# 480 columns instead of 512 for the lower half of the ninth tap, in a float32r convolution layer split over two row tiles

## The chip, the cores and the metric

The kernel runs on one core of a Trainium2 chip. The metric is the device time of one execution in microseconds. Three runs of the kernel before gave 2569.12, 2569.26 and 2569.37 us (median 2569.26). Beside them there is a profile of one execution. The mean granted clock of TensorE in it is 1.000 of full speed.

## What is computed

The input x is 4 images of 32 x 32 pixels with 16 channels. Four residual layers follow each other, each on a group-normalized x. Three of them (0, 1 and 3) are the same kind of position-dependent convolution; cut down:

```python
first   = einsum('ijyx,byxc->bijc', M, x)
kern    = G as (h*w*f, c, 3, 3)              # one 3x3 kernel for every output pixel (i,j) and f
shifted = conv(x, kern, padding='SAME')      # 1024*16 output channels over 32x32 pixels
diff    = relu(x - shifted)                  # for every (i,j): an image of 32x32
second  = einsum('ijyx,bijyxc->bijc', W, diff)
x       = x + first - second
```

Layer 3 names pixels and sums the other way round, and comes to the same work. Layer 2 is an interval network (running maxima and minima over rows and columns, two dynamic-programming steps with sigmoids, and a linear map), small beside the others.

## The kernel before

**Phases, chunks, steps.** The batch is cut into two groups of two images (g = 0, 1). A phase is one convolution layer for one group: six phases. A phase has 8 chunks of 128 output pixels (t), and a chunk has 32 steps, one for each output channel f and image b. In the very first chunk the steps are sorted by groups of four f and then by b (four steps of b = 0, then four of b = 1); in all others b changes with every step. There are 6 x 8 x 32 = 1536 steps.

**A step.** It computes, for 128 output pixels, the image x - shifted of 32 x 32 = 1024 pixels with the sign turned, in two PSUM banks of 512 columns: bank h of the pair `ps[:, h, :]` is half h of the image, 16 rows of 32 pixels. The contraction runs over 9 taps x 16 channels = 144 rows. Eight taps are spread over two slots of four taps (64 partitions each), and the ninth tap has a slot of its own. The partitions 0 to 63 and 64 to 127 hold the two halves of the image, so that each matmul has 64 rows and the two halves run on two row tiles of the systolic array. `products` (L582) issues for every weight and image operand two matmuls, h = 0 on partitions 0 to 63 and h = 1 on partitions 64 to 127; such a pair is called a pass here.

**Precision.** Weights and images are split into an upper and a lower part so that float32r products give enough of float32. In all but the first 16 steps `first_part` (L597) issues four passes (`iy` for two slots, `iz` for two slots), then ScalarE scales the two banks in place (L618). `second_part` (L621) issues two passes of `iyz` and one of the ninth tap, `im9` with `W9`. So a step has seven passes. The first 16 steps (`u < PLAIN`) use plain float32 products of `raw` for the eight taps, and float32r for the ninth.

**Order.** It is written out by hand. `conv_layer` issues the first part of step n+1, then the second part of step n. VectorE then takes min(ps, 0) times the layer's W over the 1024 columns and sums along them (L634), which gives one output column. There are four pairs of banks. In the gaps between steps, generators are advanced: `prep_parts` makes the next weights on ScalarE, VectorE and POOL and sends the halves that have to change partitions through SP's queue; `behind` does the normalization, the interval network and the image operands of the next phase.

**Image operands.** `before_conv` (L338) writes the normalized image, padded to 34 x 34, to DRAM (`xs`), and reads it back as shifted windows into `raw`, one DMA for each tap and half, both images of the group in one (L359). `RUN` is the length of such a window: 15 rows of 34 and one of 32. The ninth tap is stored four times (four rows of 16 channels) because its operand is split in precision over them. `split`, `difference`, `halve` and `halve_rest` make `iy`, `iz`, `iyz` and `im9` from it.

**The ninth tap.** It is the one at the lower right of the 3 x 3 window. For the image's last row of pixels (row 15 of half 1) it reads only the zero padding below the image.

**The start.** For phase 0 the host has laid the windows out (`xi`), not normalized. The kernel normalizes them in place (`normal`, L807) and then has to set the padding to zero again: `sides` (L794) multiplies a window's left and right column and top and bottom row by masks of 0 and 1 per partition (`kept`, made at L739 to L750 from the table `outside`), and clears the ninth tap's right column and, for half 1, its last row with memsets (L798, L799).

Of the kernel before, what the change touches and what calls it, by code (L numbers as in the profile page):

```python
# [16 lines left out]
B, H, C = 4, 32, 16  # L17
NG = 2
GB = B // NG
# [4 lines left out]
HP = H + 2  # L24
NPP = HP * HP
HI = H // 2
PITCH = HI * HP
NH = HI * H
RUN = (HI - 1) * HP + H
ROWS = P // H  # L30
FU = 4
NU = C // FU
# [9 lines left out]
def net_kernel(ctx: ExitStack, tc: tile.TileContext, x, xq, xi, convs, iv_w, iv_b, out):  # L42
# [58 lines left out]
    raws, units, chunks = {}, {}, {}  # L101
# [7 lines left out]
    def load_chunk(n):  # L109
        if n < n_chunks:  # L110
            t = n % NT
            chunks[n] = wpool.tile([P, NP], F32, tag="WT", name=f"WT_{n}")
            nc.sync.dma_start(chunks[n], convs[phases[n // NT][1]][1][t * P : (t + 1) * P, :])
# [5 lines left out]
    raw = const.tile([P, 3, GB, PITCH], F32, name="raw")  # L119
    iy = [const.tile([P, 2, GB, NH], F32R, name=f"iy{g}") for g in range(NG)]  # L120
    iz = [const.tile([P, 2, GB, NH], F32R, name=f"iz{g}") for g in range(NG)]
    iyz = [const.tile([P, 2, GB, NH], F32R, name=f"iyz{g}") for g in range(NG)]
    im9 = [const.tile([P, GB, NH], F32R, name=f"im9{g}") for g in range(NG)]
# [3 lines left out]
    first = big.tile([P, 8192], F32, tag="big", name="first")  # L127
# [3 lines left out]
    def load_plain(eng, u, at, to):  # L131
        src = convs[0][2][0, u]
        eng.dma_start(raws[u][:, ::2, at:to], src[:, :2, at:to])
        for h in range(2):
            eng.dma_start(
                raws[u][64 * h : 64 * h + 64, 1, at:to], src[64 - 64 * h : 128 - 64 * h, 0, at:to]
            )

    load_plain(nc.scalar, 0, 0, F0)
    for slot in (0, 2, 1):  # L140
        nc.sync.dma_start(raw[:, slot, 0, :RUN], xi[0][:, slot, :RUN])
    load_chunk(0)
    load_plain(nc.sync, 0, F0, FU)
    nc.sync.dma_start(raw[:, :, 1, :RUN], xi[1][:, :, :RUN])
    load_plain(nc.sync, 1, 0, FU)
# [40 lines left out]
    def image(v, x):  # L186
        return v.rearrange("... (y x) -> ... y x", x=x)[..., :H]
# [68 lines left out]
    def split(eng, g, b, name, pause=IDLE):  # L256

        high = upper(image(raw[:, :2, b], HP), 2, f"x{name}{b}")
        yield 1
        for s in range(2):  # L260
            eng.tensor_tensor(
                image(iz[g][:, s, b], H), image(raw[:, s, b], HP), image(high[:, s], H), ALU.subtract
            )
            yield pause
            nc.scalar.activation(iy[g][:, s, b], high[:, s], AF.Copy, scale=EPS)
# [72 lines left out]
    def before_conv(g, layer):  # L338
        xn = work.tile([P, NT, GC], F32, tag="xn", bufs=2, name=f"xn_{g}_{layer}")
        xns[g] = xn  # L340
        yield from group_norm(g, f"c{g}{layer}", xn, 1 if layer == 2 else 4)

        nc.vector.transpose(
            xt[g][:, :, 1 : 1 + H], xn
        )
        inner = xs[g][:, HP : HP + H * HP].rearrange("p (t r n) -> p r t n", r=ROWS, n=HP)
        for r in range(ROWS):
            nc.sync.dma_start(inner[:, r], xt[g][GC * r : GC * (r + 1)])  # L350
        yield 2
        xsv = xs[g].rearrange("(b c) n -> c b n", b=GB)
        for slot, row, tap in [(tap // 4, tap % 4, tap) for tap in range(8)] + [
            (2, row, 8) for row in range(4)
        ]:
            for h in range(2):
                off = (HI * h + tap // 3) * HP + tap % 3
                r0 = 64 * h + C * row
                nc.sync.dma_start(  # L359
                    raw[r0 : r0 + C, slot ^ h if slot < 2 else 2, :, :RUN], xsv[:, :, off : off + RUN]  # L360
                )
            yield 1
        yield 6 if layer == 2 else 12
        for b in range(GB):
            yield from split(nc.gpsimd, g, b, f"{g}{layer}")
            yield IDLE
            halve(image(im9[g][:, b], H), image(raw[:, 2, b], HP), low_x)
            for s in range(2):
                difference(nc.gpsimd, g, b, s)
            yield 3  # L370
            halve_rest(image(im9[g][:, b], H), image(raw[:, 2, b], HP), low_x)
            yield 1
# [73 lines left out]
    def interval_layer(g):  # L446
# [18 lines left out]

        raw = one[:GC].rearrange("p (j t r) -> p r t j", j=H, r=ROWS)
        for row in range(ROWS):
            if row == 2:
# [110 lines left out]
        yield 1  # L579


    def products(ps, pairs, first):  # L582


        for k, (w, v) in enumerate(pairs):
            for h in range(2):
                r = slice(64 * h, 64 * h + 64)
                nc.tensor.matmul(  # L588
                    ps[:, h, :],
                    lhsT=w[r],  # L590
                    rhs=v[r],
                    start=first and k == 0,
                    stop=k == len(pairs) - 1,
                    skip_group_check=not first,
                )

    def first_part(step):  # L597
        phase, t, f, b = step
        g = phases[phase][0]
        n = phase * NT + t  # L600
        u = n * NU + f // FU
        ps = bank_pair(f"pc_{n}_{f}_{b}")
        if u < PLAIN:
            products(
                ps,
                [(raws[u][:, s, f % FU], image(raw[:, s, b], HP)) for s in range(2)]
                + [(units[u][3][:, f % FU], im9[g][:, b])],
                True,
            )
            return ps  # L610
        WU, WL, WD, W9 = (w[..., f % FU, :] for w in units[u])
        products(
            ps,
            [(WU[:, s], iy[g][:, s, b]) for s in range(2)]
            + [(WL[:, s], iz[g][:, s, b]) for s in range(2)],
            True,
        )
        nc.scalar.activation(ps, ps, AF.Copy, scale=1.0 + EPS)  # L618
        return ps

    def second_part(step, ps):  # L621

        phase, t, f, b = step
        g = phases[phase][0]
        n = phase * NT + t
        u = n * NU + f // FU
        if u >= PLAIN:
            WU, WL, WD, W9 = (w[..., f % FU, :] for w in units[u])
            products(
                ps, [(WD[:, s], iyz[g][:, s, b]) for s in range(2)] + [(W9, im9[g][:, b])], False  # L630
            )
        col = b * C + f
        junk = work.tile([P, NP], F32, tag="junk", name=f"junk_{n}_{col}")
        nc.vector.scalar_tensor_tensor(  # L634
            junk,
            ps.rearrange("p h n -> p (h n)"),
            0.0,
            chunks[n],
            op0=ALU.min,
            op1=ALU.mult,  # L640
            accum_out=accs[phase][:, t, col : col + 1],
        )
        if (f, b) == (C - 1, GB - 1):
            acc = accs[phase][:, t]
            if n == 0:
                plain_acc = acc.rearrange("p (b c) -> p b c", c=C)[:, :, : PLAIN * FU]
                nc.vector.tensor_scalar_mul(plain_acc, plain_acc, EPS)
            if phase < len(phases) - 1:
                nc.gpsimd.tensor_scalar_mul(acc, acc, 1.0 / EPS)  # L649
                nc.gpsimd.tensor_tensor(X[g][:, t], X[g][:, t], acc, ALU.add)  # L650
            else:
                nc.vector.scalar_tensor_tensor(
                    X[g][:, t], acc, 1.0 / EPS, X[g][:, t], op0=ALU.mult, op1=ALU.add
                )
                if t == NT - 2:
                    nc.sync.dma_start(out[g][:, : NT - 1], X[g][:, : NT - 1])
# [55 lines left out]
    pairs = const.tile([P, C // 2], F32, name="pairs")  # L712
# [13 lines left out]
    for b in range(GB):  # L726
# [3 lines left out]
    rows = const.tile([P, 2, 4], F32, name="rows")  # L730
# [3 lines left out]

    outside = {
        "left0": (rows[:, 0, 0::3], rows[:, 1, 2:3]), "right0": (rows[:, 0, 2:3], rows[:, 1, 1:2]),
        "top0": (rows[:, 0, 0:3],), "bottom0": (rows[:, 1, 2:4],),
        "left1": (rows[:, 0, 2:3], rows[:, 1, 0::3]), "right1": (rows[:, 0, 1:2], rows[:, 1, 2:3]),
    }  # L739
    kept = const.tile([P, len(outside) + 4], F32, name="kept")  # L740
    keep = {}
# [23 lines left out]
    ps = bank("ps_own")  # L765
# [28 lines left out]
    def sides(eng, b, slot):  # L794

        v = raw[:, slot, b].rearrange("p (y x) -> p y x", x=HP)
        if slot == 2:
            eng.memset(v[:, :, H - 1 : H], 0.0)  # L798
            eng.memset(v[64:, HI - 1, :H], 0.0)  # L799
        for side, at in (  # L800
            ("left", v[:, :, 0]), ("right", v[:, :, H - 1]),
            ("top", v[:, 0, :H]), ("bottom", v[:, HI - 1, :H]),
        ):
            if f"{side}{slot}" in keep:
                eng.tensor_scalar_mul(at, at, keep[f"{side}{slot}"])  # L805

    def normal(eng, b, slot):  # L807
        v = raw[:, slot, b, :RUN]
        if eng is nc.scalar:
# [127 lines left out]
```

## Time and profile before

| | us |
|---|---|
| median of three runs | 2569.26 (2569.12 to 2569.37) |
| span of the profiled execution, first to last instruction | 2566.6 |
| TensorE matmuls busy (L588 and others) | 2552.4, 99% of the span |
| TensorE weight loads busy | 2064.8 |
| VectorE busy | 2079.7 |
| ScalarE busy | 1894.8 |
| POOL busy | 1102.1 |
| matmuls of the ninth tap (im, W), 3072 of them | 622.6, 396 ns each |
| matmuls of iy, iz, iyz, 6080 of each | 966 to 968 each, 392 to 393 ns each |

The profiled execution is one execution recorded by the hardware; the page gives its span, and no other total for it. What lies before the first and after the last instruction is in the timed runs but not in the span: 2569.26 - 2566.6 = 2.7 us.

How to read it: busy time of matmuls is a sum of intervals whose ends are modelled and which overlap, as two row tiles work at once and a matmul begins before the results of the last have drained. So a share of 99% doesn't say that the array is full. Starts are recorded. The distance between the starts of successive passes is therefore the measure used here. A line of the timeline merges neighbouring instructions of one kind ("x4" are two passes of two halves): its first number is the start of the first, its second the time until the end of the last. PE's weight loads (PEld) are shown apart from its matmuls. A wait is put down to the instruction whose end released it.

### The profile page before, as it was taken

Reading aid. Unit: us, or ns where it says so; the run is one execution under the profiler, and the core shown is the slowest. Engines: PE = TensorE matmul, PEld = TensorE weight load, DVE = VectorE, ACT = ScalarE, POOL = GpSimd, SP = SyncE. Lnnn points to the kernel's source line nnn. Section 1 sums busy time; section 2 is a strip of 40 time slices with the busy share of each in tenths; the row PEclk is TensorE's granted clock in tenths of the full one; section 3 lists DMA queues with packets and bytes.
Section 4 is the critical chain, followed back from the end, with each engine's and each line's share of the span. In section 5 each row is a group of like instructions: output and inputs, shape, how many; then the busy total and the mean of one; then the engine's idle time right before and its main releaser. Section 6 shows DMA issues by size and latency. Waiting matters only on the chain.

```text
span 2566.6 us, 56663 instructions
## 1 busy us (share of the span) xinstructions
PE 2552.4 (99%) x21906; PEld 2064.8 (80%) x21906; DVE 2079.7 (81%) x3620; ACT 1894.8 (74%) x2181; POOL 1102.1 (43%) x991
## 2 busy tenths in 40 slices
PE   8999999999999999999999999999999999999999
PEld 5998888888888887888888877788878887788887
DVE  9887777888777887777788888888888887777777
ACT  4777777777777777777777777777777777777776
POOL 3445333453333434333345554454646344333332
PEclk9999999999999999999999999999999999999999
DMA  5656344464444654444454444554444466344442
GB/s 170 187 144 170 108 132 140 114 167 136 128 136 128 194 159 120 136 129 128 132 140 132 132 116 133 140 156 130 122 132 133 130 161 198 110 141 132 132 132 52
DMA packets 81182, 353.80 MB, mean 138 GB/s; under 512 B 18448, under 2 KB 20368, under 8 KB 80144
## 3 DMA queue, kind: packets, MB, share of 16 engines
q1 hardware_dynamic: 79920, 349.57, 48.7%
q8 instruction: 172, 2.82, 0.4%
q14 instruction: 98, 0.80, 0.1%
q10 hardware_dynamic: 864, 0.58, 0.1%
q0 software_dynamic: 128, 0.02, 0.0%
HBM read 199.19 MB, written 0.98 MB: 78 GB/s over the span
## 4 chain that ended last, share of the span: by engine, by line
PE 99%; ACT 0%; DVE 0%; issue 0%; POOL 0%; DVEq 0%; ACTq 0%; POOLq 0%
PE pc L588 98%; PE pf L387 1%; ACT pc L618 0%; PE ps_l L510 0%; PE ps_r L523 0%; DVE junk L634 0%; ACT L323 0%; DVE raw L805 0%; PE ps_y L574 0%; DVE kept L748 0%; ACT L553 0%; PE ps_v L758 0%; DVE raw L813 0%; DVE kept L744 0%; DVE squares L781 0%
## 5 line engine op out<-in xcount | busy, mean ns | idle before, releaser
L634 DVE SCALAR_TENSOR_TENSOR junk<-pc,WT 128x1024 f32<-128x1024 f32 x1536 | 1879.7, 1224 | 461.7 <-PE pc L588 416.2
L618 ACT ACTIVATE pc<-pc 128x1024 f32<-128x1024 f32 x1520 | 1531.8, 1008 | 637.2 <-PE pc L588 607.4
L588 PE MATMUL pc<-iyz,parts 64*128 64x512 f32 x6080 | 966.5, 393 | 1.7 <-ACT pc L618 1.7
L588 PE MATMUL pc<-iy,parts 64*128 64x512 f32 x6080 | 967.8, 393 | 0.0
L588 PE MATMUL pc<-iz,parts 64*128 64x512 f32 x6080 | 965.3, 392 | 0.0
L227 POOL TENSOR_TENSOR parts<-raw,upper_w 128x512 fp32r<-128x512 f32 x190 | 246.0, 1295 | 1040.6 <-PE pc L588 892.7
L588 PEld LDWEIGHTS pc<-iyz,parts 64*128 64x128 f32 x6080 | 583.0, 185 | 133.8 <-ACT pc L618 5.5
L588 PEld LDWEIGHTS pc<-iy,parts 64*128 64x128 f32 x6080 | 582.3, 185 | 132.5 <-issue 4.4
L588 PEld LDWEIGHTS pc<-iz,parts 64*128 64x128 f32 x6080 | 584.0, 185 | 128.6
L588 PE MATMUL pc<-im,W 64*128 64x512 f32 x3072 | 622.6, 396 | 0.0
L588 PEld LDWEIGHTS pc<-im,W 64*128 64x128 f32 x3072 | 295.4, 185 | 68.6 <-issue 3.5
L228 POOL TENSOR_TENSOR W<-W,raw 128x512 fp32r<-128x512 f32 x190 | 248.0, 1305 | 2.0 <-ACT W L169 1.9
L231 POOL TENSOR_TENSOR parts<-parts 128x512 fp32r<-128x512 f32 x190 | 247.0, 1300 | 2.7 <-ACT parts L226 2.5
L204 POOL TENSOR_TENSOR raw<-raw,ident 128x512 f32<-128x512 f32 x190 | 201.0, 1058 | 41.7 <-DMA raw<-in_g 39.1
L169 ACT ACTIVATE W<-raw,low_w 128x512 fp32r<-128x512 f32 x190 | 136.1, 716 | 0.1
L634 DVE DVE_READ_ACCUMULATOR junk<-pc,WT 128x1 f32 x1536 | 127.4, 83 | 0.0
L226 ACT ACTIVATE parts<-upper_w 128x512 fp32r<-128x512 f32 x190 | 118.5, 624 | 4.2 <-DVE upper_w L193 4.2
L230 ACT CAST parts<-upper_w 128x512 fp32r<-128x512 f32 x190 | 116.8, 615 | 0.0
L649 POOL TENSOR_SCALAR acc<-acc 128x32 f32<-128x32 f32 x40 | 11.5, 288 | 170.4 <-DVE junk L634 165.8
L193 DVE TENSOR_SCALAR upper_w<-raw 128x512 int32<-128x512 int32 x190 | 82.1, 432 | 0.2
L542 POOL TENSOR_TENSOR tables<-ft_b,rt 128x1089 f32<-128x1089 f32 x16 | 37.7, 2354 | 0.5 <-DVE s_b L549 0.5
L542 POOL TENSOR_TENSOR tables<-ft_a,rt 128x1089 f32<-128x1089 f32 x16 | 37.7, 2356 | 0.0
(140 smaller groups left out, 393.8 us busy)
## 6 DMA issues: line engine op xcount, KB each, us to landing
raw<-in_g SPq DMA_DIRECT2D x190, 768.0 KB, 7.2
parts<-parts SPq DMA_DIRECT2D x380, 384.0 KB, 5.0
WT<-in_w SPq DMA_DIRECT2D x48, 512.0 KB, 4.6
MT<-in_mt SPq DMA_DIRECT2D x6, 2048.0 KB, 12.8
raw<-xs SPq DMA_DIRECT2D x120, 67.8 KB, 2.4
raw<-in_xi SPq DMA_DIRECT2D x3, 271.0 KB, 4.6
raw<-in_xi SPq DMA_DIRECT2D x1, 813.0 KB, 6.1
xs<-xt SPq DMA_DIRECT2D x20, 34.0 KB, 2.3
```

The costliest lines, as they stand in the source:

```text
L169: nc.scalar.activation(dst, src, AF.Copy, scale=mask[:, 1:2])
L193: nc.vector.tensor_scalar(t.bitcast(I32), src.bitcast(I32), HIGH, None, op0=ALU.bitwise_and)
L204: eng.tensor_tensor(raws[u][:, s, at:to], raws[u][:, s, at:to], pick[s][:, f0 + at : f0 + to].unsqueeze(2).to_broadcast([P, to - at, P]), ...
L226: nc.scalar.activation(WD, high, AF.Copy, scale=-EPS)
L227: nc.gpsimd.tensor_tensor(WL, w8, high, ALU.subtract)
L228: nc.gpsimd.tensor_tensor(W9, W9.bitcast(F32), src[:, 2], ALU.add)
L230: nc.scalar.copy(WU, high)
L231: nc.gpsimd.tensor_tensor(WD, WD.bitcast(F32), WL.bitcast(F32), ALU.add)
L542: nc.gpsimd.tensor_tensor(t, ft[:, i, :].unsqueeze(1).to_broadcast([P, T1, T1]), rt, ALU.add,)
L588: nc.tensor.matmul(ps[:, h, :], lhsT=w[r], rhs=v[r], start=first and k == 0, stop=k == len(pairs) - 1, skip_group_check=not first,)
L618: nc.scalar.activation(ps, ps, AF.Copy, scale=1.0 + EPS)
L634: nc.vector.scalar_tensor_tensor(junk, ps.rearrange("p h n -> p (h n)"), 0.0, chunks[n], op0=ALU.min, op1=ALU.mult, accum_out=accs[phase][ ...
```

## The change

The ninth tap's matmul for half 1 of the image takes the first 15 rows only: `LAST` = 15 x 32 = 480 columns. The columns 480 to 511 of that bank then hold what the other eight taps gave.

Which half runs on which row tile now depends on the image: for b = 0 as before, for b = 1 partitions 0 to 63 hold half 1 and partitions 64 to 127 hold half 0 (`half = h ^ b`). So the matmul of 480 columns is on the second row tile for b = 0 and on the first for b = 1. The windows that are read from DRAM, and the host's layout for phase 0, follow: within one DMA the two images are now 16 padded rows further or nearer to each other (`window`). The masks at the start follow too: for slot 0, top and bottom rows are masked for b = 0 only, for slot 1 for b = 1 only, which makes two more masks; the memset of the ninth tap's last row is left out.

In the first 16 steps the plain passes and the ninth tap's pass are issued by two calls of `products` in place of one; the order of the matmuls is the same.

```diff
@@ -27,6 +27,7 @@
 PITCH = HI * HP
 NH = HI * H
 RUN = (HI - 1) * HP + H
+LAST = (HI - 1) * H
 ROWS = P // H
 FU = 4
 NU = C // FU
@@ -350,14 +351,22 @@
             nc.sync.dma_start(inner[:, r], xt[g][GC * r : GC * (r + 1)])
         yield 2
         xsv = xs[g].rearrange("(b c) n -> c b n", b=GB)
+
+        def window(h, tap):
+
+            off = (HI * h + tap // 3) * HP + tap % 3
+            v = xsv[:, :, off : off + RUN]
+            (c, nc_), (b, nb), (n, nn) = v.ap
+            b += (HI if h == 0 else -HI) * HP
+            return bass.AP(v.tensor, v.offset, [[c, nc_], [b, nb], [n, nn]])
+
         for slot, row, tap in [(tap // 4, tap % 4, tap) for tap in range(8)] + [
             (2, row, 8) for row in range(4)
         ]:
             for h in range(2):
-                off = (HI * h + tap // 3) * HP + tap % 3
                 r0 = 64 * h + C * row
                 nc.sync.dma_start(
-                    raw[r0 : r0 + C, slot ^ h if slot < 2 else 2, :, :RUN], xsv[:, :, off : off + RUN]
+                    raw[r0 : r0 + C, slot ^ h if slot < 2 else 2, :, :RUN], window(h, tap)
                 )
             yield 1
         yield 6 if layer == 2 else 12
@@ -579,16 +588,18 @@
         yield 1
 
 
-    def products(ps, pairs, first):
+    def products(ps, b, pairs, first, last=True):
 
 
         for k, (w, v) in enumerate(pairs):
             for h in range(2):
                 r = slice(64 * h, 64 * h + 64)
+                half = h ^ b
+                n = LAST if k == len(pairs) - 1 and last and half else NH
                 nc.tensor.matmul(
-                    ps[:, h, :],
+                    ps[:, half, :n],
                     lhsT=w[r],
-                    rhs=v[r],
+                    rhs=v[r] if n == NH else v[r][:, :n],
                     start=first and k == 0,
                     stop=k == len(pairs) - 1,
                     skip_group_check=not first,
@@ -602,18 +613,17 @@
         ps = bank_pair(f"pc_{n}_{f}_{b}")
         if u < PLAIN:
             products(
-                ps,
-                [(raws[u][:, s, f % FU], image(raw[:, s, b], HP)) for s in range(2)]
-                + [(units[u][3][:, f % FU], im9[g][:, b])],
-                True,
+                ps, b, [(raws[u][:, s, f % FU], image(raw[:, s, b], HP)) for s in range(2)],
+                True, last=False,
             )
+            products(ps, b, [(units[u][3][:, f % FU], im9[g][:, b])], False)
             return ps
         WU, WL, WD, W9 = (w[..., f % FU, :] for w in units[u])
         products(
-            ps,
+            ps, b,
             [(WU[:, s], iy[g][:, s, b]) for s in range(2)]
             + [(WL[:, s], iz[g][:, s, b]) for s in range(2)],
-            True,
+            True, last=False,
         )
         nc.scalar.activation(ps, ps, AF.Copy, scale=1.0 + EPS)
         return ps
@@ -627,7 +637,7 @@
         if u >= PLAIN:
             WU, WL, WD, W9 = (w[..., f % FU, :] for w in units[u])
             products(
-                ps, [(WD[:, s], iyz[g][:, s, b]) for s in range(2)] + [(W9, im9[g][:, b])], False
+                ps, b, [(WD[:, s], iyz[g][:, s, b]) for s in range(2)] + [(W9, im9[g][:, b])], False
             )
         col = b * C + f
         junk = work.tile([P, NP], F32, tag="junk", name=f"junk_{n}_{col}")
@@ -734,8 +744,9 @@
 
     outside = {
         "left0": (rows[:, 0, 0::3], rows[:, 1, 2:3]), "right0": (rows[:, 0, 2:3], rows[:, 1, 1:2]),
-        "top0": (rows[:, 0, 0:3],), "bottom0": (rows[:, 1, 2:4],),
+        "top00": (rows[:, 0, 0:3],), "bottom00": (rows[:, 1, 2:4],),
         "left1": (rows[:, 0, 2:3], rows[:, 1, 0::3]), "right1": (rows[:, 0, 1:2], rows[:, 1, 2:3]),
+        "top11": (rows[:, 1, 0:3],), "bottom11": (rows[:, 0, 2:4],),
     }
     kept = const.tile([P, len(outside) + 4], F32, name="kept")
     keep = {}
@@ -796,13 +807,12 @@
         v = raw[:, slot, b].rearrange("p (y x) -> p y x", x=HP)
         if slot == 2:
             eng.memset(v[:, :, H - 1 : H], 0.0)
-            eng.memset(v[64:, HI - 1, :H], 0.0)
         for side, at in (
-            ("left", v[:, :, 0]), ("right", v[:, :, H - 1]),
-            ("top", v[:, 0, :H]), ("bottom", v[:, HI - 1, :H]),
+            (f"left{slot}", v[:, :, 0]), (f"right{slot}", v[:, :, H - 1]),
+            (f"top{slot}{b}", v[:, 0, :H]), (f"bottom{slot}{b}", v[:, HI - 1, :H]),
         ):
-            if f"{side}{slot}" in keep:
-                eng.tensor_scalar_mul(at, at, keep[f"{side}{slot}"])
+            if side in keep:
+                eng.tensor_scalar_mul(at, at, keep[side])
 
     def normal(eng, b, slot):
         v = raw[:, slot, b, :RUN]
@@ -879,11 +889,11 @@
     xi = np.zeros((GB, 2, 3, 4, C, PITCH), np.float32)
     for h in range(2):
         for tap in range(9):
-            off = (HI * h + tap // 3) * HP + tap % 3
             rows = slice(None) if tap == 8 else tap % 4
             slot = 2 if tap == 8 else tap // 4 ^ h
-            v = xp[:, :, off : off + RUN]
-            xi[:, h, slot, rows, :, :RUN] = v[:, None] if tap == 8 else v
+            for b in range(GB):
+                off = (HI * (h ^ b) + tap // 3) * HP + tap % 3
+                xi[b, h, slot, rows, :, :RUN] = xp[b, :, off : off + RUN]
     give("xi", xi.transpose(0, 1, 3, 4, 2, 5).reshape(GB, P, 3, PITCH))
     layers = [("L0_conv", "W"), ("L1_conv", "W"), ("L3_conv", "Wp")]
     for n, (pre, w) in enumerate(layers):
```

## The prediction, made before the changed kernel was run

> **What bounds the kernel now.** I read the page from the top: busy shares, then the chain that ended last, then the costliest groups.
>
> ```profile
> PE 2552.4 (99%) x21906; PEld 2064.8 (80%) x21906; DVE 2079.7 (81%) x3620; ACT 1894.8 (74%) x2181; POOL 1102.1 (43%) x991
> ...
> PE 99%; ACT 0%; DVE 0%; issue 0%; POOL 0%; DVEq 0%; ACTq 0%; POOLq 0%
> PE pc L588 98%; PE pf L387 1%; ACT pc L618 0%; PE ps_l L510 0%; PE ps_r L523 0%; DVE junk L634 0%; ACT L323 0%; DVE raw L805 0%; PE ps_y L574 0%; DVE kept L748 0%; ACT L553 0%; PE ps_v L758 0%; DVE raw L813 0%; DVE kept L744 0%; DVE squares L781 0%
> ...
> L634 DVE SCALAR_TENSOR_TENSOR junk<-pc,WT 128x1024 f32<-128x1024 f32 x1536 | 1879.7, 1224 | 461.7 <-PE pc L588 416.2
> L618 ACT ACTIVATE pc<-pc 128x1024 f32<-128x1024 f32 x1520 | 1531.8, 1008 | 637.2 <-PE pc L588 607.4
> ...
> L588 PE MATMUL pc<-im,W 64*128 64x512 f32 x3072 | 622.6, 396 | 0.0
> ```
>
> A busy PE proves little, since ends of matmuls are modelled. But the chain runs through L588 for 98% of the span, and DVE (416.2 us) and ACT (607.4 us) idle waiting for it. So TensorE's own pace is the bound. The next question is what sets that pace: columns, weight loads, or the pairing of the two halves. The timeline of PE in a quiet stretch gives it:
>
> ```profile
> 1300.17 0.63 PE L588 MATMUL pc<-iy,parts 64*128 64x512 f32 x4
> 1300.64 0.63 PE L588 MATMUL pc<-iz,parts 64*128 64x512 f32 x4
> 1301.10 0.63 PE L588 MATMUL pc<-iyz,parts 64*128 64x512 f32 x4
> 1301.57 0.40 PE L588 MATMUL pc<-im,W 64*128 64x512 f32 x2
> 1301.81 0.63 PE L588 MATMUL pc<-iy,parts 64*128 64x512 f32 x4
> ```
>
> A step (one f, one b) is seven passes, a pass two matmuls of 64 rows, one on each row tile. From iy to iy is 1301.81 - 1300.17 = 1.64 us; the single records repeat 1631 and 1636 ns, so a pass is 233.4 ns and a step 1633.5.
>
> **Weight loads do not set it.** Each load normally begins 2 ns after its tile's matmul. In one place it waited for ACT and came late (timelines of the weight loads and of PE):
>
> ```profile
> 1341.92 0.38 PEld L588 LDWEIGHTS pc<-iyz,parts 64*128 64x128 f32 x4
> ```
> ```profile
> 1341.64 0.63 PE L588 MATMUL pc<-iz,parts 64*128 64x512 f32 x4
> 1342.11 0.63 PE L588 MATMUL pc<-iyz,parts 64*128 64x512 f32 x4
> ```
>
> The second iz pass starts at 1341.88, the load 46 ns after it, and still the two passes take 0.47 us, as elsewhere. So a load has at least 44 ns to spare: what a pass must wait for is the matmul before it on the same row tile.
>
> **The row tiles are not locked together.** In most passes the two halves start 3 to 4 ns apart. But from 45 us to 250 us tile 1 trails by 27 to 30 ns (pairs shown as 0.42 where others have 0.39 or 0.40) at the same pace:
>
> ```profile
> 99.79 0.42 PE L588 MATMUL pc<-iy,parts 64*128 64x512 f32 x2
> 100.02 0.66 PE L588 MATMUL pc<-iz,parts 64*128 64x512 f32 x4
> ```
>
> If tile 1 waited only for tile 0 it would catch up; it doesn't, so it is held by its own 233.4 ns. The interval network shows it more strongly, where ps_r (rows 0 to 63 only) gives tile 0 extra work:
>
> ```profile
> 1382.77 0.39 PE L588 MATMUL pc<-im,W 64*128 64x512 f32 x1
> 1382.77 0.50 PE L588 MATMUL pc<-iy,parts 64*128 64x512 f32 x1
> 1383.00 0.25 PE L523 MATMUL ps_r<-tables,r 64*128 64x110 f32 x1
> ```
>
> Tile 1 takes up the next step's iy before tile 0 has reached the ps_r that stands ahead of it in the program.
>
> **What the Trainium skill says.** "TensorE: Matmul & The Clock Gate", section Back-to-back issue gap: a warm matmul of N columns follows another after N/2.4 + 2.5 ns. The float32 records here agree (a plain raw product shows as two records of 429 ns, 2 x 512/2.4 + 2.5 = 429.2); the float32r pass of 512 doesn't: 233.4 against 215.8, and the measurement decides. The column price, 1/2.4 = 0.417 ns, I take from it. Same page, The mechanism: tiles overlap with starts about 4 ns apart (agrees), and matmuls are strictly in order (the iy above starts ahead of ps_r, so across row tiles this trace differs). "TensorEngine Tiling (Array Packing)", Key Properties: tiles operate independently (agrees); its Gotcha 1: two row tiles must not use one PSUM bank at once, which the change keeps, since both swap banks together.
>
> **The change part by part.** (1) 480 columns instead of 512. The ninth tap's product of the lower half loses 32 columns in each of 1536 steps: on tile 1 for b = 0, on tile 0 for b = 1. Each tile so gets 1536/2 = 768 shortened passes. One saves 32 x 0.417 = 13.3 ns, if the 20.1 ns by which a pass exceeds its columns (233.4 - 213.3) are fixed; if they grow with the columns, 233.4 x 32/512 = 14.6 ns. No shorter float32r pass is in the trace, so this is bounded from 0 (a fixed slot) to 14.6; I take 13.3, since float32 records show a fixed remainder. Sum: 768 x 13.3 = 10.2 us (11.2 at the other end), all on the path. For b = 0 tile 1 runs up by 13 ns, for b = 1 tile 0: the distance between the tiles swings and neither runs away, except in the first chunk, sorted four f at a time by b (53 ns).
>
> (2) Turning the tiles between the two banks with b: no instruction is added; the order on PE stays. A tile already goes to another pair of banks every three or four passes, with no step in the 233 ns. Cost 0; upper bound under the rivals.
>
> (3) Splitting products for the first 16 steps leaves the same matmuls; they have 480 columns too and are in the 768.
>
> (4) Start: kept gets two more sums. They lie in the chain ahead of the first matmul (DVE, L744 to L750, 2.7 to 4.4 us), at 0.06 us each: three take 0.19. +0.13 us. The two 64x32 memsets go (POOL, 0.12 us, beside PE's first matmuls; one DVE in step one's shadow): 0, and 0.1 at most. The top and bottom multiplications of batch 1 move from slot 0 to slot 1, two each as before: 0.
>
> (5) DMA: the window's batch stride has another sign and size, with 24 issues a layer and 67.8 KB each as before; one pair of issues per fetch changes its place against a wait for POOL's zero rows, done hundreds of us earlier. Normalization begins in the phase before, and conv loads of the next phase do not stand in the chain. Cost 0, cover: the rest of a phase of some 430 us (2566.6 over six phases).
>
> What is late next? ACT ends its 1008 ns at 1302.31, and the weight load that waits for it starts at 1302.51: 190 ns in hand, plus the 44 above. The change takes at most 15 of it. DVE has 0.41 us of idle a step. Neither takes over.
>
> Sum: span 2566.6 - 10.2 + 0.13 = 2556.5. The profiled execution has no separate total; around its span the timed runs have 2569.26 - 2566.6 = 2.7 us, start and end, which stay. So 2559.2 us, 0.39% below the median; at 14.6 ns 2558.2.
>
> **Rivals.** Pair as a slot: both halves are dispatched together and the longer sets the pass. For it: starts 3 to 4 ns apart nearly everywhere, and a full 512 always stands beside the 480. Against: the two stretches above. Time 2569.26 + 0.13 = 2569.4. Chance 0.10.
>
> Half taken: the tiles may part by only some ns before the order of dispatch holds the front one, so that of a swing of 13 ns about half is used. For it: the distance falls back to 3 ns after each stall. Against: 30 ns kept for 200 us. Time 2569.3 - 5.1 + 0.1 = 2564.3. Chance 0.05.
>
> Slower: the turn costs. At every change of b each tile starts on the other bank of a pair; if that start is not hidden it would cost once more what a pass has beyond its columns, 20.1 ns. 1536 x 20.1 = 30.9, less 10.2: 2569.3 + 20.7 + 0.1 = 2590.1. It decides from 6.6 ns a turn (half of 13.3, as there are two steps for one saving). For it: before, a tile never writes both banks of a pair. Against: under (2). Chance 0.05.
>
> **How the numbers follow.** Forecast 0.80, at 2559.2, its own range 2557.0 (some 1 us under the 14.6 case, for waits that move) to 2561. What a measurement can tell is about 0.2%, 5.1 us. Faster by more: 0.80 and half of the middle case, 0.82; within: 0.10 and the rest, 0.13 rounded up; slower 0.05. For 8 in 10 the range goes from 2557.0 to 2564.6, the half-taken case included; out are 0.15 and the forecast's own tails.
>
> **What would show it.** Right: im in two forms of 64x512 and 64x480, 1536 each; a step pair of 3254 ns instead of 3267; starts of the two tiles 3 ns apart in some steps and 16 in others; ACT's and DVE's idle time before L618 and L634 lower by some 10 us; the first matmul 0.13 us later. Wrong: step pairs still of 3267 ns (slot), or a first iy pass after a turn that comes later than 233 ns (turn).

## The result and the profile after

The changed kernel takes 2549.96 us (median of 5 runs, 2549.48 to 2551.40); the kernel before 2569.12 us in the same session (5 runs). The ratio is 0.9926, 95% interval [0.9913, 0.9938]. So it is faster by 19.2 us, where 10.1 us were forecast (2559.2, range 2557.0 to 2564.6). The direction and the place were right; the size was off by a factor of nearly two, and the time lies below the range.

The page of the changed kernel, the lines that answer to those of before:

```profile
span 2548.2 us, 56662 instructions
...
PE 2533.8 (99%) x21906; PEld 2182.0 (86%) x21906; DVE 2079.2 (82%) x3621; ACT 1893.1 (74%) x2181; POOL 1103.8 (43%) x990
...
PE 99%; ACT 0%; DVE 0%; issue 0%; POOL 0%; DVEq 0%; ACTq 0%; POOLq 0%
...
L644 DVE SCALAR_TENSOR_TENSOR junk<-pc,WT 128x1024 f32<-128x1024 f32 x1536 | 1880.1, 1224 | 444.1 <-PE pc L599 404.3
L628 ACT ACTIVATE pc<-pc 128x1024 f32<-128x1024 f32 x1520 | 1531.8, 1008 | 621.9 <-PE pc L599 597.2
...
L599 PE MATMUL pc<-im,W 64*128 64x512 f32 (+1 forms) x3072 | 631.9, 390 | 0.0
```

Apart from TensorE's pace little has moved. The span falls by 18.4 us; VectorE's and ScalarE's instructions last as long as before, and the idle time in front of them shrinks by 17.6 us (461.7 to 444.1) and 15.3 us (637.2 to 621.9). The chain is still TensorE. No wait has taken the place of another. The weight loads (PEld) are busy for 2182.0 us instead of 2064.8 though there are as many and one takes 185 ns as before. Their busy time counts loads that overlap once, and where the two tiles lie further apart it is higher: between 100 and 200 us, with the tiles 41 to 73 ns apart, it is 99.4 us; before, at 30 ns, it was 91.6.

Where in the step the time went shows in the timeline of PE, at a place where the tiles lie apart:

```profile
101.25 0.45 PE L599 MATMUL pc<-im,W 64*128 64x512 f32 x2
101.48 0.67 PE L599 MATMUL pc<-iy,parts 64*128 64x512 f32 x4
101.95 0.67 PE L599 MATMUL pc<-iz,parts 64*128 64x512 f32 x4
102.42 0.67 PE L599 MATMUL pc<-iyz,parts 64*128 64x512 f32 x4
102.88 0.44 PE L599 MATMUL pc<-im,W 64*128 64x480 f32 x2
103.10 0.69 PE L599 MATMUL pc<-iy,parts 64*128 64x512 f32 x4
103.55 0.40 PE L599 MATMUL pc<-iz,parts 64*128 64x512 f32 x1
```

The first number of a line is here always tile 0. From im at 101.25 to im at 102.88 it makes seven passes in 1.63 us, as before: in this step the short matmul is on tile 1. Then its own short pass: 102.88 to 103.10 is 0.22 us, and the two iy passes that follow take 0.45 instead of 0.47. The single records give 217, 228 and 226 ns for these three; before, three passes took 700. So 29 ns went at once: 16 in the short pass and 13 in the two full passes behind it. The later alternation of 231 and 236 ns takes back 2. The time from a step to the next but one is 3240.0 ns in the quiet stretches, 3266.7 before: 26.7 ns for a shortened pass, exactly twice its 13.3 ns of columns.

### The profile page after: what moved, and what is told of

Its sections match the earlier page's. It is cut to its first block, busy times and chain, and to the rows that moved or that the text cites. A ratio compares the mean times of both kernels' runs of the same rounds, so it can differ in the third digit from the quotient of the medians.

```text
span 2548.2 us, 56662 instructions
## 1 busy us (share of the span) xinstructions
PE 2533.8 (99%) x21906; PEld 2182.0 (86%) x21906; DVE 2079.2 (82%) x3621; ACT 1893.1 (74%) x2181; POOL 1103.8 (43%) x990
## 4 chain that ended last, share of the span: by engine, by line
PE 99%; ACT 0%; DVE 0%; issue 0%; POOL 0%; DVEq 0%; ACTq 0%; POOLq 0%
PE pc L599 98%; PE pf L396 1%; ACT pc L628 0%; PE ps_l L519 0%; PE ps_r L532 0%; DVE junk L644 0%; ACT L562 0%; ACT L324 0%; DVE raw L815 0%; PE ps_y L583 0%; DVE kept L759 0%; DVE kept L755 0%; PE ps_v L769 0%; DVE raw L823 0%; DVE squares L792 0%
## 5 line engine op out<-in xcount | busy, mean ns | idle before, releaser
L644 DVE SCALAR_TENSOR_TENSOR junk<-pc,WT 128x1024 f32<-128x1024 f32 x1536 | 1880.1, 1224 | 444.1 <-PE pc L599 404.3
L628 ACT ACTIVATE pc<-pc 128x1024 f32<-128x1024 f32 x1520 | 1531.8, 1008 | 621.9 <-PE pc L599 597.2
L599 PE MATMUL pc<-iyz,parts 64*128 64x512 f32 x6080 | 990.7, 393 | 1.8 <-ACT pc L628 1.8
L599 PE MATMUL pc<-iz,parts 64*128 64x512 f32 x6080 | 989.8, 392 | 0.0
L599 PEld LDWEIGHTS pc<-iyz,parts 64*128 64x128 f32 x6080 | 622.6, 185 | 96.7 <-ACT pc L628 5.6
L599 PEld LDWEIGHTS pc<-iz,parts 64*128 64x128 f32 x6080 | 619.9, 185 | 92.3
L599 PEld LDWEIGHTS pc<-iy,parts 64*128 64x128 f32 x6080 | 615.3, 185 | 90.2 <-issue 4.4
L599 PE MATMUL pc<-im,W 64*128 64x512 f32 (+1 forms) x3072 | 631.9, 390 | 0.0
L599 PEld LDWEIGHTS pc<-im,W 64*128 64x128 f32 x3072 | 315.3, 185 | 49.8 <-issue 3.2
```

The lines of the kernel that those rows point to most:

```text
L599: nc.tensor.matmul(ps[:, half, :n], lhsT=w[r], rhs=v[r] if n == NH else v[r][:, :n], start=first and k == 0, stop=k == len(pairs) - 1, ski ...
L644: nc.vector.scalar_tensor_tensor(junk, ps.rearrange("p h n -> p (h n)"), 0.0, chunks[n], op0=ALU.min, op1=ALU.mult, accum_out=accs[phase][ ...
```

## The experiments

The measure for each is the median and its ratio to the kernel before, and, more sharply, the mean time of a step in the quiet stretches of the trace (from the starts of the last ninth-tap matmuls; 1633.33 ns before, 1620.00 with the change). "Saved" is per shortened pass. A column is 0.4167 ns, as in the prediction, and what a pass takes beyond its columns (20.0 ns at 512) is called the remainder.

### Which part of the change it is

`swap_512`: the change's layout and turn, full columns. The memset of the ninth tap's last row is back too, since those columns are read again; so it is in all the runs below that have the turn, but for `bf16_swap_480`. The diffs show the lines that matter; `...` stands for the lines between them.

```diff
-                n = LAST if k == len(pairs) - 1 and last and half else NH
+                n = NH
...
+            eng.memset(v[64 * (1 - b) : 64 * (2 - b), HI - 1, :H], 0.0)
```

> The halves turn row tiles with the batch as in the change, but the ninth tap keeps 512 columns in both halves. Theory L (length: the whole gain, 26.7 ns a shortened pass, comes from the shorter pass itself): no change, 2569.3 us, im passes 233 ns apart. Theory T (turn: half of the 19 us comes from the tiles changing banks with the batch): about 2560 us.

Measured: 2569.18 us, ratio 1.0000 [0.9991, 1.0009], step 1633.33 ns. The turn gives nothing and costs nothing. Theory T and my slower rival (a price of 20 ns a turn) both fall.

`tile1_480`: the kernel before with

```diff
+                n = 480 if last and h == 1 and k == len(pairs) - 1 else NH
...
-                    ps[:, h, :],
+                    ps[:, h, :n],
...
-                    rhs=v[r],
+                    rhs=v[r] if n == NH else v[r][:, :n],
```

> No turn: half 1 of the ninth tap stays on row tile 1 and has 480 columns in every step. Independent row tiles (my prediction and theory L): tile 0 still has seven full passes a step, so no gain, 2569.1 us; tile 1 gets ahead until the order of dispatch holds it. Theory S (the tiles share something, so that a column saved on either helps both): the same gain as the change, about 2550 us.

Measured: 2568.93 us, ratio 0.9999 [0.9990, 1.0007], step 1633.33 ns (tile 0's). The columns saved on one tile alone are worth nothing; theory S falls. The timeline shows tile 1 ahead:

```profile
501.42 0.38 PE L589 MATMUL pc<-im,W 64*128 64x480 f32 x1
501.64 0.39 PE L589 MATMUL pc<-iy,parts 64*128 64x512 f32 x1
501.65 0.39 PE L589 MATMUL pc<-im,W 64*128 64x512 f32 x1
501.87 0.41 PE L589 MATMUL pc<-iy,parts 64*128 64x512 f32 x2
```

Tile 1 starts the next step's iy (501.64) when tile 0 starts its im (501.65): it has run up by a whole pass. There it is held: from 275 to 490 us, some 130 steps, its ninth tap is never more than 270 ns ahead, though every step has 13.3 ns of columns less. So the turn isn't a gain, but it is what makes columns count that are saved in one half only.

`both_480`: as the last, with both halves cut (`if last and k == len(pairs) - 1`).

> No turn, 480 columns in both halves of the ninth tap (this leaves out the ninth tap for row 15 of the upper half). Every tile then has one short pass in each step, 1536 instead of 768. Theory L: twice the gain of the change, 1536 x 26.7 ns = 41 us, 2528 us. Theory T: only the columns, 1536 x 13.3 = 20.4 us, 2548.7 us. Theory S: 2528 to 2550 us.

Measured: 2539.54 us, ratio 0.9884 [0.9869, 0.9899], step 1613.33 ns: 20.0 ns saved for each short pass, now one in seven. More than the columns, less than the 26.7 ns of the change. The numbers of theories L and T (2528 and 2548.7) are not met; S's range (2528 to 2550) holds the time, but S has fallen above.

`six_480`: as the last, with six of seven passes cut.

> Six of a step's seven passes, and the ninth tap's of the first 16 steps, have 480 columns in both halves (this leaves out the last 32 columns of those products in each half). Theory L in its plain form (every pass of 480 takes 206.7 ns where one of 512 takes 233.4): 1520 x 6 x 26.7 = 243 us, 2326 us. Theory E (edge: only the change from a long to a short pass gives the extra 13.3 ns): 1520 x (80 + 13.3) = 142 us, 2427 us. A fixed remainder: 122 us, 2447 us. A rate: 133 us, 2436 us.

Measured: 2439.31 us, ratio 0.9492 [0.9478, 0.9507]. Steps are less even here: tile 0's take 1544.1 ns from 275 to 1270 us in quiet stretches, and 1538.1 ns from 2190 to 2400 us, which gives 89.2/6 = 14.9 and 95.2/6 = 15.9 ns a short pass. So where nearly all passes are short, each saves its columns and 1.5 to 2.5 ns. Theory L falls: "a pass of 480 is 26.7 ns faster than one of 512" is false as a rule, and the saving hangs on the passes around it. Theory E's 93.3 ns a step lie between the two values; but E gives 26.7 ns a step for `both_480`, where 20.0 were measured, and so falls there. The whole time is nearest to the rate (2436), by luck as far as the runs tell, since a rate would give 14.6 ns everywhere.

### How it depends on the cut

In the layout of the change, `LAST` replaced by 496, 448 and 384:

```diff
-                n = LAST if k == len(pairs) - 1 and last and half else NH
+                n = 496 if k == len(pairs) - 1 and last and half else NH
```

> As the change, but 496 columns in the ninth tap's lower half: 16 columns less than full instead of 32. The change saved 26.7 ns a shortened pass, twice its 13.3 ns of columns. Theory D (double: every column off saves its own time and as much of the remainder, until the remainder of 20 ns is gone): 13.3 ns, 768 x 13.3 = 10.2 us, 2559.1 us. Theory J (jump: any shortening saves its columns and 13.3 ns once): 6.7 + 13.3 = 20 ns, 15.4 us, 2553.9 us. Fixed remainder: 5.1 us, 2564.2 us.

> 448 columns, 64 less than full (this leaves out the ninth tap for row 14 of the lower half). Theory D: 26.7 ns of columns and at most the remainder of 20 ns: 46.7 ns, 35.8 us, 2533.5 us. Theory J: 26.7 + 13.3 = 40 ns, 30.7 us, 2538.6 us. Fixed remainder: 20.5 us, 2548.8 us.

> 384 columns, 128 less than full (this leaves out the ninth tap for rows 12 to 14 of the lower half). Theory D: 53.3 + 20 = 73.3 ns, 56.3 us, 2513 us. Theory J: 53.3 + 13.3 = 66.7 ns, 51.2 us, 2518.1 us. If the weight load of the next pass (106 to 183 ns after its start) begins to hold a pass that has 160 ns of columns, less than either.

| columns in the one short pass of 14 | median us | ratio | saved, ns | columns' part, ns | beyond them, ns |
|---|---|---|---|---|---|
| 496 | 2557.24 | 0.9952 [0.9936, 0.9969] | 20.0 or 6.7 | 6.7 | 13.3 or 0 |
| 480 (the change) | 2549.96 | 0.9926 [0.9913, 0.9938] | 26.7 | 13.3 | 13.3 |
| 448 | 2546.55 | 0.9911 [0.9897, 0.9926] | 30.0 | 26.7 | 3.3 |
| 384 | 2525.57 | 0.9829 [0.9814, 0.9843] | 60.0 | 53.3 | 6.7 |

Theory D falls (it wanted 13.3 and 46.7 ns at 496 and 448) and so does theory J (40 at 448). At 384 columns, less was saved than either wanted, which the expectation gave as the sign of a late weight load; but at 448, too, less was saved than they wanted, so this does not show one. What is saved beyond the columns neither grows nor shrinks steadily with the cut. And it has two values within one run: the kernel with 496 columns, PE's timeline at 100 us and at 500 us:

```profile
99.83 0.52 PE L599 MATMUL pc<-im,W 64*128 64x496 f32 x2
100.06 0.76 PE L599 MATMUL pc<-iy,parts 64*128 64x512 f32 x4
100.52 0.76 PE L599 MATMUL pc<-iz,parts 64*128 64x512 f32 x4
...
103.09 0.52 PE L599 MATMUL pc<-im,W 64*128 64x496 f32 x2
```
```profile
502.29 0.40 PE L599 MATMUL pc<-im,W 64*128 64x496 f32 x2
502.51 0.65 PE L599 MATMUL pc<-iy,parts 64*128 64x512 f32 x4
502.97 0.66 PE L599 MATMUL pc<-iz,parts 64*128 64x512 f32 x4
...
505.54 0.40 PE L599 MATMUL pc<-im,W 64*128 64x496 f32 x2
```

In the first stretch, with the tiles 130 ns apart (0.52 us for a pair of 0.39), im to im over two steps is 103.09 - 99.83 = 3.26 us (3260 ns in the records: the columns alone), and the records show even distances of 233 and 234 ns. At 502 us, with the tiles nearer to each other, it is 505.54 - 502.29 = 3.25 us (3247 ns in the records, as in most of the run from 250 us on), and passes alternate between 231 and 236 ns. Same instructions, same operands, another price.

The distance between the tiles doesn't decide it. Around 76 us tile 1 lies 24 to 59 ns behind tile 0 and takes 3260 ns while tile 0 beside it takes 3247; around 1100 us it lies 14 to 40 ns behind, and both take 3247. What goes with the price in this run is the tile's own rhythm. In an even rhythm the short pass takes 227 ns and the passes behind it 233 again (tile 1 at 76 us). In the alternating one the short pass takes 224 and the two full ones behind it 228 and 226 (tile 0 there). Of tile 0's pairs of steps with an even rhythm 179 of 183 take 3260 ns; of those with an alternating one 1130 of 1204 take 3246 or 3247. What puts a tile into one rhythm or the other isn't shown. Nor is the rhythm alone the price: before the change tile 0 has both, and both take 3267 ns.

`both_496`: both halves of the ninth tap at 496, no turn.

> No turn, 496 columns in both halves of the ninth tap (this leaves out half of row 15 of the upper half in it). With 480 columns such a step lost 20.0 ns[...]; with 496 in one half and the turn it was 20.0 or 6.7 ns a shortened pass. Phase theory (a pass's remainder depends on where it falls in a pattern[...]): not in proportion, some multiple of 8 clocks between 16 and 48, 6.7 to 20 ns a step, 2539 to 2559 us. Fixed remainder: 6.7 ns, 2559.1 us. Rate: 7.3 ns, 2558.2 us.

Measured: 2558.46 us, ratio 0.9958 [0.9944, 0.9972], step 1626.67 ns: 6.7 ns, the columns and nothing more, where 480 in the same place saved 20.0. Most of its passes alternate too, so an alternating rhythm doesn't always bring the extra.

### Whose remainder it is

`solo_512` and `solo_480`: of row tile 1 only the first and last pass of each group; in the second, tile 0's ninth tap has 480 columns.

```diff
+                if h and not (first and last) and 0 < k < len(pairs) - 1:
+                    continue
+                n = 480 if last and h == 0 and k == len(pairs) - 1 else NH
```

> All passes of 512 columns, but row tile 1 issues only four of a step's seven (this leaves out three products of the image's lower half); tile 0 issues all seven. Theory X (the remainder of 20 ns comes from the two row tiles getting into each other's way): three of seven passes of tile 0 run alone and lose up to 20 ns each, 1520 x 60 = 91 us, 2478 us. Theory O (it comes from a row tile's own work): no change, 2569.4 us.

> As the run with tile 1 thinned out, and tile 0's ninth tap has 480 columns in every step (this leaves out row 15 of the upper half in it as well). Theory O: beside its own partner without the cut, the same 20.0 ns a step as with both halves cut, 1536 x 20 = 30.7 us less. Theory X: 13.3 ns a step, 20.5 us less.

Measured: 2569.21 us, ratio 1.0000 [0.9991, 1.0008], step 1633.33 ns; and 2539.14 us, ratio 0.9883 [0.9868, 0.9898], step 1613.33 ns in the quiet stretches. So both the remainder of 20 ns and the 20.0 ns saved are the same beside a neighbour that issues four of seven passes. In the trace of `solo_512`, from 60 to 760 us, 316 of tile 0's passes have none of tile 1's beside them and 848 have one nearly all the way (a pass of tile 1 is counted as 233 ns, and longer where its record is longer). Both kinds take 233.4 ns in the mean. Theory X falls: the remainder of a full pass is the row tile's own affair.

`four_m96`: 512 columns, four of seven passes with 96 weight columns.

```diff
+                m = 96 if (k or not first) and k < len(pairs) - 1 and not (first and last) else P
...
-                    ps[:, h, :],
-                    lhsT=w[r],
+                    ps[:m, h, :],
+                    lhsT=w[r] if m == P else w[r][:, :m],
```

> Passes of 512 columns throughout, but four of a step's seven passes load 96 weight columns instead of 128 (this leaves out 32 of 128 output pixels of these products). Theory W (the remainder of 20 ns is the weight load taking read slots from the moving columns, in proportion to its columns): a quarter of 20.1 ns a pass, 4 x 5 ns x 1520 = 30.5 us, 2538.8 us. If the remainder has nothing to do with the load's size: no change, 2569.3 us.

Measured: 2558.95 us, ratio 0.9959 [0.9944, 0.9973], step 1626.67 ns: 6.7 ns a step, in the mean 1.7 ns for a pass with a quarter fewer weight columns, where theory W wanted 5; the case of no change (2569.3) falls too. So the number of weight columns has a part in the remainder, but no proportional one. The edit narrows the load and what the pass writes (96 of 128 output pixels) alike, and which of the two gave the 1.7 ns isn't shown. The Trainium skill, "TensorE: Matmul & The Clock Gate", section Step-by-step: what each phase is for, says that loading the next weights takes no read bandwidth from the running matmul; here fewer weight columns made the stream of passes 6.7 ns a step shorter, so the pass is not free of them; whether reads are the reason no run shows.

`bf16`: the operands read as the upper two of each four bytes, outside the first 16 steps.

```diff
+                wr, vr = w[r], v[r]
+                if not (first and last):
+                    wr = wr.bitcast(mybir.dt.bfloat16)[:, 1::2]
+                    vr = vr.bitcast(mybir.dt.bfloat16)[:, 1::2]
...
-                    lhsT=w[r],
-                    rhs=v[r],
+                    lhsT=wr,
+                    rhs=vr,
```

> All passes of 512 columns, but outside the first 16 steps weights and images are read as the upper two bytes of each four (bfloat16), so that the lower bits of every operand are left out. If the remainder belongs to reading four bytes a column: passes of about 216 ns, 7 x 17.6 x 1520 = 187 us, 2382 us. If it belongs to row tiles or to weight loads of 128 columns as such: 2569 us.

Measured: 2499.60 us, ratio 0.9729 [0.9715, 0.9744], between the two expectations. A pass is 226.7 ns, a remainder of 13.3 instead of 20.0. The loads are shorter too (its groups; before, 185 ns each):

```profile
L592 PEld LDWEIGHTS <-parts 64*128 64x128 bf16 x18240 | 949.6, 93 | 1125.8 <-issue 12.3 <-DMA parts<-parts 1.4
L592 PEld LDWEIGHTS <-W 64*128 64x128 bf16 x3040 | 160.1, 93 | 186.9
```

Two things changed at once here, the load and the width of a column, so it says only that a third of the remainder goes away with the four-byte operands.

### Place and distance

All with the turn, full columns but for the named cut of 480.

```diff
 pos_480
+                n = 480 if len(pairs) == 4 and k == 2 and half else NH
 sparse_480 (cut = f % 2 == 0)
+                n = 480 if cut and last and k == len(pairs) - 1 and half else NH
 pair_480
+                n = 480 if last and k > 0 and k >= len(pairs) - 2 and half else NH
```

> The turn as in the change, but the 480 columns are in the first iz pass of the first part instead of the ninth tap (this leaves out one row of that product in the lower half). Theory M (memory: any short pass among long ones also brings the next two passes forward, 26.7 ns in all): 1520/2 x 26.7 = 20.3 us, 2549 us. Theory Y (the extra belongs to the place: two iy passes follow, the first of which starts a bank anew): columns alone, 10.1 us, 2559 us.

> As the change, but only for even f, so that a row tile has one short pass in 28 (the odd ones do the full 512). If one in fourteen is already far enough apart: half the gain of the change, 384 x 26.7 = 10.2 us, 2559 us. If the saving still grows with distance: more; at 33 ns 12.8 us, 2556.5 us.

> The turn; 480 columns in the lower half of the ninth tap and of the iyz pass just ahead of it, so that a row tile has two short passes in a row once in fourteen (this leaves out one row of that iyz product). Memory of two to three passes: the first of the pair gives little more than its columns and the second the full 26.7 ns, about 41 ns, 31.5 us, 2537.8 us. If each gives the full saving: 53.4 ns, 41 us, 2528.3 us. Columns alone: 20.5 us, 2548.8 us.

`pos_480`: 2549.76 us, ratio 0.9924 [0.9910, 0.9939], step 1620.00 ns. The same 26.7 ns in another place: theory Y falls, nothing hangs on the ninth tap or on the iy passes behind it. `sparse_480`: 2559.33 us, ratio 0.9962 [0.9947, 0.9976], step 1626.67 ns in the quiet stretches, which is 26.7 ns for each short pass, one in 28. So one in 14 is far enough apart. `pair_480`: 2549.36 us, ratio 0.9924 [0.9909, 0.9938], step 1620.00 ns. Two short passes in a row save 26.7 ns together, exactly their columns, and no more than one alone. Of its three expectations "columns alone" (2548.8) is met; theory M's 41 ns and the full saving twice (53.4) are not. Its timeline:

```profile
599.96 0.66 PE L599 MATMUL pc<-iy,parts 64*128 64x512 f32 x4
...
602.99 0.40 PE L599 MATMUL pc<-im,W 64*128 64x480 f32 x2
603.20 0.42 PE L599 MATMUL pc<-iy,parts 64*128 64x512 f32 x2
```

603.20 - 599.96 = 3.24 us from iy to iy over two steps, as in the change, though twice as many columns are gone.

`bf16_swap_480`: the change, with the operands of `bf16`.

> The change with weights and images of all passes outside the first 16 steps read as the upper two bytes of each four (bfloat16; the lower bits of every operand are left out). Without the cut that took 2499.6 us and passes were an even 226.7 ns. If the extra hangs on the four-byte weight loads: columns alone, 10.2 us, 2489.4 us. If it is there with any load: 20 us, 2479 us. This is also the fastest version that these runs point to.

Measured: 2487.16 us, ratio 0.9681 [0.9667, 0.9696]. It is 12.4 us under `bf16`. Against 1586.67 ns there, a step takes 1578.33 ns in most quiet stretches, 16.7 ns a short pass: the columns and 3.3 ns. From 550 to 840 us it takes 1580.00, 13.3 ns a short pass: the columns alone. So the extra is smaller here, and again it has two values within one run; the median is too near to "columns alone" (2489.4) to tell them apart. It leaves out the lower bits of the operands, so it is no replacement for the change in a kernel that splits its operands to keep them.

## Why the prediction was right in its direction and wrong in its size

**The bound and the independent tiles: right.** TensorE's chain set the end, and each row tile runs at its own pace until it is about one pass ahead: no gain from one tile alone, no change beside a thinned-out neighbour. The rivals "pair as a slot" (2569.4) and "half taken" (2564.3) fall: nearly every pair of steps in the quiet stretches has the full saving, whether the tiles are 20 or 70 ns apart. The distance between them swings as forecast, though not between 3 and 16 ns only: at 500 us tile 1 is between 19 ns behind tile 0 and 19 ns ahead of it.

**The weight load isn't late, but it isn't free.** From the load that came 46 ns late I concluded that a pass waits only for the matmul before it. In the streams of passes no run speaks against that; yet the number of weight columns is in the pass's length (1.7 ns in the mean for 32 less, with the narrower output that goes with them).

**The term that failed** is in part (1): "One saves 32 x 0.417 = 13.3 ns, if the 20.1 ns by which a pass exceeds its columns (233.4 - 213.3) are fixed; if they grow with the columns, 233.4 x 32/512 = 14.6 ns", and "bounded from 0 (a fixed slot) to 14.6". It measured 26.7 ns over two steps. The term charged the saving to the shortened pass and left every full pass at 233.4 ns. The runs show that the full passes behind it get shorter too: at 102.88 us the short pass lost 16 ns and the two behind it 13. I had two forms for how one pass depends on its columns and took them for the two ends. But a remainder that I could not explain had no reason to keep its size, in that pass or in the next. With room for the whole remainder once, 13.3 + 20.1 = 33.4 ns, 25.7 us, the low end would have been 2543.7 us and the range would have held the time; but the trace of before does not make that a bound either. The price of a full float32 record ("since float32 records show a fixed remainder") was taken from another kind of pass.

**What the remainder is** the runs settle in part. In full passes it is a row tile's own; it isn't the turn or the place; it gets smaller with fewer weight columns and with two-byte operands; and it isn't a fixed sum or a share of the columns. Around single short passes it fell, over two steps, by 0 or 13.3, 13.3, 3.3 and 6.7 ns for 496, 480, 448 and 384 columns, in an order that doesn't follow the cut, and with 496 it took two values along with the tile's own rhythm. All step times in quiet stretches but those of `six_480` are whole multiples of 4 columns' time (1.67 ns), most of 16 (6.7 ns). I take it that a pass's start falls into some slot of a pattern, so that a shift of 13 ns can be worth 27 or 13; that is argued from the numbers, not shown, and what makes the pattern, and with it the cause of the extra, stays open.

**The sum.** 768 x 26.7 = 20.5 us; 18.4 us were seen in the span. Step by step against the kernel before, the saving is 13.3 ns a step nearly everywhere, with breaks (2.1 us in all) at these places:
- The start. The two added sums put the first matmul at 9.92 us instead of 9.80, 0.12 us later; 0.13 was forecast.
- The granted clock. The record of the clock has its rise to full speed at 14.16 us instead of 12.64, and matmuls until then took twice as long (starts of raw matmuls 853 ns apart before it, 429 after): 0.65 us were lost between the first and third step. It rises between 12.6 and 16.0 us in the eighteen profiles of this case, and at 15.25 us in `tile1_480`, whose start is that of the kernel before; so nothing shows it to be an effect of the change.
- The first chunk apart from that, some 0.2 us, and three other groups of 64 steps, two of them with the first terms (pf), 0.04 us each.
- The steps from 768 to 1280, with the interval networks, where waits pace a part of the steps: 0.65 us. A further 0.4 us are missing between steps 1280 and 1344; I have not traced these to an instruction.

The start of the chain in the changed kernel, with the two sums that were added (x2 in place of one piece):

```profile
4.05 0.16 DVE kept L759
4.21 0.14 DVE kept L755 x2
...
4.38 0.17 DVE kept L761
...
9.92 1.22 PE pc L599
```

**The zero-cost edits** (DMA windows, the order of two issues, the split of `products`) were right: `swap_512` has them all and its time can't be told from before. (It also has the 0.13 us at the start, which is too little to be seen.)

**The margin behind it** was right too. PE's waits for ACT are still six, 1.8 us in all where they were 1.7.

## What to carry to other kernels

When one resource paces a kernel, an instruction's price can hang on the ones around it. Where a part of it can't be explained, give the range room for that part, in the shortened instruction and in those behind it, and time a cut in the very sequence where it will stand: the same 32 columns were worth 0 on one tile alone, 13.3 ns each in two passes in a row, 14.9 or 15.9 in six of seven, 20.0 in one of seven and 26.7 in one of fourteen. With two row tiles, cut both or take turns: what is saved on one alone is lost. Take the distance between starts as the measure, and the mean over a whole period, not the busy time of a matmul (im went from 396 to 390 ns of "busy" while two steps lost 26.7).

## What the runs showed that I had not expected

A float32r pass of 512 columns and 128 weight columns on one of two row tiles takes 233.3 ns at full clock, whether the other tile is running a pass or not; read as the upper two bytes of the same four it takes 226.7. Passes next to a short one change their length (228 and 226 ns), and the sum over a period is what is steady; part of what a cut saves is saved in the passes behind it. A row tile can start a pass a whole pass ahead of the other, past matmuls that stand earlier in the program. And two adjacent cuts of 32 columns saved exactly as much as one.
